# A graph attention kernel: how a small vector reaches its place, where a pass's first products and additions stand, and the order of eight banks

## The chip, the cores and the metric

The kernel runs on one core of one Trainium2 chip. The core has a matrix engine (PE, with its weight loads shown as PEld), a vector engine (DVE), a scalar engine (ACT), GpSimd (POOL) and a queue engine for transfers (SP). Each runs its own list of instructions in order, and they wait for each other through semaphores. The metric is the device time of one execution in microseconds (us). The kernel before took 2859.95 us, the median of three runs between 2857.50 and 2861.08.

## The reference

Two layers over 4096 nodes with 256 features. Each is a residual around a graph operation on h = relu(layernorm(x)).

```python
# layer 0: graph attention, 4 heads of 64
h = (h @ W).reshape(n, heads, head_dim)
src = einsum('nhd,d->nh', h, a[:head_dim, 0]);  dst = einsum('nhd,d->nh', h, a[head_dim:, 0])
e = src[:, :, None] + dst.T[None, :, :]
e = where(e > 0, e, 0.2 * e);  e = where(adj > 0, e, NEG_INF)
out = einsum('nhm,mhd->nhd', softmax(e), h)
x = x + layernorm(out) * gamma + beta
# layer 1: two steps of Xf = R @ Xf (R = row-normalised adj + I) and
# Xa = top_p(softmax(q k^T)) @ Xa, then x = x + layernorm(h + Z) * ln_g + ln_b
```

## The kernel before

Rows are taken in 32 blocks of 128. X, the features, stays on the chip. Layer 0 has two stages, both with the order of instructions written out by hand (`manual_schedule`).

**The prologue** goes through the 32 blocks once. For a block, DVE takes the row statistics (`measured`, L149 and L150), POOL makes scale and bias from them (`steps`, L141 to L144), ACT normalises and clips (`opened`, L244, hb), PE transposes (`turned_rows`, L251), ACT copies the transposes (L255, hT), and PE multiplies by wx (`multiplied`, L258). ACT and DVE then turn the product into weighted rows in three bfloat16 parts (`read`, `weighed`, `first_part`, `left`, `second_part`, `third_part`), of which the first head's stay on the chip (ut0) and the others are stored. `turn_of(b)` issues one step for several blocks at once, so that the engines overlap.

The tile wx holds W and, in its last 8 columns, W times the two halves of the vector a placed head by head. These columns are a product of w_t, the transpose of W (L575, copied at L576), and spots (L582). The tile spots is zero but for a's two halves, one column for each half and head; it is filled by four transfers issued on ACT's queue (L201), which are laid out one element per partition. Issues for the weights of layer 1 (L207 to L209) stand behind them on the same queue, and hb of block 0 behind those.

**The passes.** There are 16: four groups of eight row blocks, and in each group four heads, so that pass k belongs to group k // 4 and head k % 4. A pass has 16 pairs of source blocks. For a pair, ACT or DVE makes signs (`signs`, L371 and L373), DVE makes two masks from the signs and the adjacency (`masks`, L379 and L380), and PE adds four products for each of eight banks, 32 in all (`products`, L399). A bank is one accumulator `acc` for one row block. Signs are issued three pairs ahead of the products, and masks two. At the start of the next pass the banks are evicted, one after another, by ACT (L413) and DVE (L416), and PE begins the new pass's products into a bank once it has been read. Work that follows from an eviction (division, row statistics, the residual and the store of a finished group) is put in a list `later` and taken one piece per pair; the group's end (`closing`) falls into the next group's first-head pass.

The residual needs x + beta. The 32 additions of beta to a block of X are done on POOL (L612) during first-head passes. POOL also issues the transfers of the adjacency (L175, L551), in order with its other work.

The first pair of pass 0 stands at the end of the prologue. Its eight banks are those that the prologue uses for its own products, and one of them, bank 7, first serves to transpose the 128 source terms (`spread_all`, L564, copied at L565 into sT).

After the last pass `passing.close()` gives the eight banks back and new pools take them. PE goes on with the first hop of layer 1 (L630), then logits (L736) and attention products (L1104).

Of the kernel before, what the change touches and what calls it, by code (L numbers as in the profile page):

```python
# [11 lines left out]
F32 = mybir.dt.float32  # L12
# [14 lines left out]
P = 128  # L27
# [13 lines left out]
G0 = 8  # L41
# [15 lines left out]
def gat_then_top_p_diffusion(  # L57
# [18 lines left out]
    nc = tc.nc  # L76
    N, D = x.shape
    HD = a.shape[0] // 2
    H = D // HD
    DA = w2_t.shape[0]  # L80
    NB = N // P
    KC = D // P
# [11 lines left out]
    ident = const.tile([P, P], F32, name="ident")  # L94
# [62 lines left out]
    W3 = 3 * W1  # L157
# [4 lines left out]
    with tc.tile_pool(name="l0", bufs=1) as l0, tc.tile_pool(name="l0s", bufs=2) as l0s, tc.tile_pool(name="l0o", bufs=1) as l0o:  # L162
        passing = ctx.enter_context(ExitStack())
        l0a, l0u, l0m = (passing.enter_context(tc.tile_pool(name=x, bufs=n)) for x, n in (("l0a", 9), ("l0u", 6), ("l0m", 3)))
        pools = SimpleNamespace()
# [18 lines left out]
        def in_bank(i, shape):  # L184
            return pools.ps0.tile(shape, F32, name=f"b{i}", tag=f"acc{i}")
# [3 lines left out]
        with tc.manual_schedule(engines=every | {ET.SP}):  # L189
            wx = rp.tile([P, KC, D + 2 * H], F32, name="wx", tag="ar", bufs=4)  # L190
# [6 lines left out]
            nc.sync.dma_start(X[:, 0, :], x[:P, :])  # L197
            spots = l0.tile([P, KC, 2, H], F32, name="spots")
            nc.vector.memset(spots, 0.0)
            for h in range(H):  # L200
                nc.scalar.dma_start(spots[ds(h * HD % P, HD), h * HD // P, :, h],  # L201
                                    bass.AP(tensor=a.tensor, offset=a.offset, ap=[[1, HD], [HD, 2]]))
            nc.sync.dma_start(wx[:, :, :D], w.rearrange("(k p) d -> p k d", p=P))
            nc.sync.dma_start(X[:, 1:4, :], x[P:4 * P, :].rearrange("(b p) d -> p b d", p=P))
            for g in range(1, NB // 4):
# [20 lines left out]
            def measured(b):  # L226
                if b < NB:
                    if b % 4 == 0:
                        pro.mv = l0s.tile([P, 4, nc.vector.BN_AGGR_DIM], F32, name="mv4")
                    moments_of(pro.mv[:, b % 4, :], X[:, b, :])  # L230
                    if b == 0:
                        pro.first = [l0s.tile([P, 4], F32, name=f"{x}4") for x in ("rs", "nmr")]
                    if b < 2:
                        steps(pro.mv[:, ds(b, 1)], 1, l0s, *(t[:, ds(b, 1)] for t in pro.first))
                    if b == 3:
                        steps(pro.mv[:, 2:], 2, l0s, *(t[:, 2:] for t in pro.first))
                    elif b % 4 == 3:
                        pro.scales[b // 4] = steps(pro.mv, 4, l0s)
# [21 lines left out]
            def read(b):  # L260
                pm, uv = pro.pm[b], uvs[b % len(uvs)]
                for t, scale in enumerate((1.0, ALPHA)):
                    nc.scalar.activation(uv[:, :, t, HD:], pm[:, ds(D + H, H)][:, :, None], AF.Exp, scale=scale)
                nc.vector.tensor_scalar(sd_c[:, :, :, b], pm[:, ds(D, 2 * H)].rearrange("p (t h) -> p t h", t=2),
                                        TINY, -TINY, ALU.add, ALU.add)
# [77 lines left out]
                    mask_stage(0)  # L343

        PAIRS = NB // 2
        passes = [(ig, h) for ig in range(NB // G0) for h in range(H)]
        shared = {}
        out_rows = {}
        later = []
        lifted = list(range(NB))  # L350
# [38 lines left out]

        def products(k, p, m, banks=range(G0)):  # L390
            ig, h = passes[k]
            if p == 0 and banks[0] == 0:
                shared[k].acc = [pools.ps0.tile([P, 2, W3 + 1], F32, name=f"acc{i}") for i in range(G0)]
            cols = W3 + (h == 0)
            for i in banks:
                for c in range(2):
                    j = 2 * p + c
                    for t in range(2):
                        nc.tensor.matmul(shared[k].acc[i][:, t, :cols], m[t][:, c, ts(i, P)],  # L399
                                         shared[k].ut[j // QUARTER][:, j % QUARTER, t, :cols],  # L400
                                         start=(j == 0 and t == 0), stop=(j == NB - 1 and t == 1))

        def evacuate(k):
            ig, h = passes[k]
            acc = shared[k].acc
            if h == 0:
                out_rows[ig] = l0o.tile([P, G0, D], F32, name="o")
            st = l0o.tile([P, 4, 2 * H * (W3 + 1) // 2], F32, name="st").rearrange("p a b -> p (a b)")
            st = st[:, :G0 * 2 * W3].rearrange("p (i t k d) -> p i t k d", i=G0, t=2, k=3)
            for i in range(G0):  # L410
                b = ig * G0 + i
                one, two = (st[:, i, t].rearrange("p k d -> p (k d)") for t in range(2))
                nc.scalar.activation(two, acc[i][:, 1, :W3], AF.Copy, scale=e_c[1][:, h, b:b + 1])  # L413
                if h == 0:
                    nc.vector.reduce_sum(rinv[:, b:b + 1], acc[i][:, :, W3], axis=AX.X)
                nc.vector.scalar_tensor_tensor(one, acc[i][:, 0, :W3], e_c[0][:, h, b:b + 1], two, ALU.mult, ALU.add)  # L416

            def three():
                for n in (1, 2):
                    nc.vector.tensor_tensor(st[:, :, 0, 0], st[:, :, 0, 0], st[:, :, 0, n], ALU.add)  # L420

            def divided():
                rden = small.tile([P, G0], F32, name="rden")
                nc.vector.reciprocal(rden, st[:, :, 0, 0, HD])
                nc.vector.tensor_mul(out_rows[ig][:, :, ts(h, HD)], st[:, :, 0, 0, :HD],
                                     rden[:, :, None].to_broadcast([P, G0, HD]))
                if h == 0:
                    rs = rinv[:, ts(ig, G0)]
                    nc.vector.tensor_scalar(rs, rs, 1.0, None, ALU.add)
                    nc.vector.reciprocal(rs, rs)  # L430
            def sourced(n):
                source(hop1, n)
                split(hop1, n + 1)

            ready = []
            if k == H + 1:
                ready = [lambda n=n: sourced(n) for n in range(LOOK + 1)]
            elif k == H + 2:
                ready = [lambda n=n: edge(hop1, n) for n in range(LOOK)]
            elif k == 2 * H + 1:  # L440
                ready = [lambda n=n: own(hop1, n + 1) for n in range(LOOK)]
            return [three, divided] + ready + (closing(ig) if h == H - 1 else [])

        PASSES = NB // G0
        S = SimpleNamespace(spare=None)

        order = [(p, j) for p in range(PASSES) for j in range(NB)]

# [70 lines left out]

        todo = [(k, p) for k in range(len(passes)) for p in range(PAIRS)]  # L520
        gs, ms = {}, {}
# [47 lines left out]
        rest.update({5 + i: lambda i=i: factors(i) for i in range(2)})  # L569
        with tc.manual_schedule(engines=every):  # L570
            measured(0)
            pt = in_bank(0, [P, KC, KC, P])
            for k in range(KC):
                for c in range(KC):
                    nc.tensor.transpose(pt[:, k, c, :], wx[:, k, ts(c, P)], ident)  # L575
            nc.vector.tensor_copy(w_t, pt)  # L576
            opened(0)
            turned_rows(0)
            pm = in_bank(1, [P, KC, 2 * H])
            for k in range(KC):  # L580
                for c in range(KC):
                    nc.tensor.matmul(pm[:, k, :], w_t[:, k, c, :], spots[:, c].rearrange("p t h -> p (t h)"),  # L582
                                     start=(c == 0), stop=(c == KC - 1))
            for b in range(1, 4):
                measured(b)
            nc.vector.tensor_copy(wx[:, :, D:], pm)
            for b in range(4, 8):
                measured(b)
            opened(1)
            for b in range(NB):  # L590
                turn_of(b)
            read(NB - 1)
            weighed(NB - 1)
            mask_stage(1)
            signed(3)
            sign_stage(2)
            for n, (k, p) in enumerate(todo):
                if n > 0 and p == 0:
                    later.extend(evacuate(k - 1))
                sign_stage(n + 3)  # L600
                mask_stage(n + 2)
                if n == 0:
                    products(k, p, ms[n], range(5))
                    spread_all()
                    products(k, p, ms.pop(n), range(5, G0))
                else:
                    products(k, p, ms.pop(n))
                if n in rest:
                    rest[n]()
                if k % H == 0 and (2 if k else 7) < p < PAIRS - 1 and lifted:  # L610
                    b = lifted.pop(0)
                    nc.gpsimd.tensor_tensor(X[:, b, :], X[:, b, :], beta_r, ALU.add)  # L612
                if 1 < p < PAIRS - 3 and later:
                    later.pop(0)()
            later.extend(evacuate(k))
# [739 lines left out]
    for n in range(STEPS):  # L1355
# [4 lines left out]
        with tc.manual_schedule(engines=every):  # L1360
# [66 lines left out]
            r = blocks[NB - 1]  # L1427
# [49 lines left out]
```

## Time and profile before

| | |
|---|---|
| median of three runs | 2859.95 us |
| the profiled execution | 2860.89 us |
| its span | 2859.1 us |
| prologue, until the first product of pass 0 | 0 to 85.4 us |
| the 16 passes, about 43.8 us each | 85.4 to 786.1 us |
| layer 1, until the end | from 787.1 us |
| longest waits of PE | L258 for ACT's hT, 20.1 us in 19 waits; L575 for wx, 4.8 us |

The profile shows one execution. The span is the time between its first and last instruction. An engine's busy time is summed over its instructions; in the timeline a row gives its start, duration, engine, line, the tiles written and read, and in square brackets the idle time just before it with what ended that. A name such as ACTq or SPq is the queue in which that engine issues transfers. Equal instructions that follow each other are merged into one row with their count. Where several conditions end a wait, it is put down to the one that came last by the profile, which can be wrong where that engine had long been done.

### The profile page before, as it was taken

How to read it: one execution, taken by the hardware profiler on the slowest of the kernel's cores; microseconds unless marked ns; L12 is line 12 of the kernel's file. 1: busy time of each engine (PE TensorE's matmuls, PEld its weight loads, DVE VectorE, ACT ScalarE, POOL GpSimd, SP SyncE). 2: the span in 40 equal slices, each digit the busy share in tenths (PEclk: the TensorE clock that was granted, in tenths of full speed). 3: DMA queues.
4: the chain of work that ended last, by engine and by line, in shares of the span. 5: the costliest groups of instructions: out<-in, count | busy, mean ns of one | idle time of the engine just before them, and what ended most of it. 6: DMA issues, size and time to landing. Idle time of an engine off the chain costs nothing. (4 is left out here: it accounts for less than half of the span.)

```text
span 2859.1 us, 51521 instructions
## 1 busy us (share of the span) xinstructions
PE 2798.3 (98%) x18789; PEld 2438.7 (85%) x18789; DVE 2167.1 (76%) x5064; ACT 1919.8 (67%) x3065; POOL 870.5 (30%) x1815
## 2 busy tenths in 40 slices
PE   6999999999999999999999999999999999999998
PEld 4899999999978788888888888667778888888887
DVE  8867868778554384888888887333564999999997
ACT  7867876879533636788778884233627778877782
POOL 7402121011000121222332221000204766666664
PEclk8999999999999999999999999999999999999999
DMA  9969696686376783000000001667991111111110
GB/s 198 252 246 194 219 235 187 219 198 223 130 242 196 236 300 94 20 20 20 25 22 20 20 20 59 226 200 237 326 337 50 31 33 39 31 31 31 36 35 26
DMA packets 190811, 376.43 MB, mean 132 GB/s; under 512 B 18768, under 2 KB 143568, under 8 KB 186448
## 3 DMA queue, kind: packets, MB, share of 16 engines
q1 hardware_dynamic: 147104, 275.31, 29.2%
q0 software_dynamic: 21504, 83.89, 12.3%
q10 hardware_dynamic: 21936, 13.79, 1.5%
q8 instruction: 153, 2.51, 0.4%
q14 instruction: 114, 0.93, 0.1%
HBM read 305.48 MB, written 113.57 MB: 147 GB/s over the span
## 5 line engine op out<-in xcount | busy, mean ns | idle before, releaser
L1104 PE MATMUL acc<-X,eT 128*128 128x256 f32 x4096 | 971.7, 382 | 3.4 <-ACT eT L1098 2.8
L1104 PEld LDWEIGHTS acc<-X,eT 128*128 128x128 f32 x4096 | 738.2, 190 | 111.2 <-ACT eT L1098 31.7
L399 PE MATMUL acc<-ut,m 128*128 128x195 bf16 (+1 forms) x8192 | 698.7, 246 | 1.9 <-DVE st L416 1.4
L399 PEld LDWEIGHTS <-m 128*128 128x128 fp8e4 x8192 | 695.9, 97 | 4.6 <-DVE st L416 1.8
L373 ACT ACTIVATE g<-sr,d_big 128x1024 uint8<-128x1024 f32 x448 | 472.7, 1136 | 3.4 <-DVE m L379 3.4
L919 ACT ACTIVATE e<-mm,nm 128x1024 f32<-128x1024 f32 x256 | 286.3, 1118 | 200.6 <-PE mm L736 199.3
L1098 ACT COPY eT<-tp 128x512 f32<-128x512 f32 x512 | 297.2, 582 | 89.6 <-PE tp L1096 89.5
L1005 DVE MAX8 cand<-big 128x8 f32<-128x228 f32 (+1 forms) x1152 | 348.3, 380 | 0.0
L630 PE MATMUL mm<-ar,hl 128*128 128x512 f32 x844 | 341.1, 407 | 6.4 <-DMA ar<-adj_d 3.0
L987 DVE SCALAR_TENSOR_TENSOR big<-e,c 128x4096 f32<-128x4096 f32 x58 | 261.9, 4515 | 97.4 <-POOL c L972 58.6
L630 PE MATMUL acc<-ar,hl 128*128 128x512 f32 x844 | 328.7, 392 | 2.5 <-DVE stage L640 1.3
L943 POOL TENSOR_TENSOR sums<-sums 128x2 f32<-128x2 f32 x64 | 12.9, 202 | 1022.4 <-ACT void L926 1022.4
L1096 PE MATMUL tp<-ident,e 128*128 128x128 f32 x2048 | 306.1, 272 | 1.9 <-DVE ns_i_u L892 1.0
L1096 PEld LDWEIGHTS tp<-ident,e 128*128 128x128 f32 x2048 | 254.8, 140 | 61.2 <-DVE ns_i_u L892 1.3
L379 DVE TENSOR_TENSOR m<-g,ax 128x512 uint32<-128x512 uint32 x256 | 180.7, 706 | 110.1 <-PE acc L399 91.4
L1030 DVE SCALAR_TENSOR_TENSOR e<-e,found 128x4096 f32<-128x4096 f32 x58 | 259.2, 4468 | 0.0
L926 ACT ACTIVATE void<-e,c1x 128x2048 int8<-128x2048 f32 x128 | 257.5, 2011 | 1.3 <-DMA ar<-adj_d 0.9
L926 ACT ACTIVATE void<-e,c 128x2048 int8<-128x2048 f32 x128 | 257.5, 2012 | 0.0
L736 PE MATMUL mm<-kT,qT 128*128 128x512 f32 x512 | 198.4, 468 | 3.5 <-ACT e L919 2.5
L380 DVE TENSOR_TENSOR m<-m,ax 128x512 uint32<-128x512 uint32 x256 | 180.4, 705 | 25.3
L630 PEld LDWEIGHTS mm<-ar,hl 128*128 128x128 f32 x844 | 158.9, 188 | 45.5 <-issue 5.7
L630 PEld LDWEIGHTS acc<-ar,hl 128*128 128x128 f32 x844 | 158.9, 188 | 40.0 <-issue 4.9
(305 smaller groups left out, 3518.6 us busy)
## 6 DMA issues: line engine op xcount, KB each, us to landing
ar<-adj_d SPq DMA_DIRECT2D x211, 512.0 KB, 4.5
adj_d<-ax POOLq DMA_DIRECT2D x32, 2048.0 KB, 7.2
ut<-uv_d SPq DMA_DIRECT2D x60, 784.0 KB, 5.9
aru<-adj_d SPq DMA_DIRECT2D x45, 512.0 KB, 4.4
ax<-in_adj_t_dram POOLq DMA_DIRECT2D x32, 512.0 KB, 18.2
x<-xf_d SPq DMA_DIRECT2D x78, 128.0 KB, 4.9
xf<-xft_d SPq DMA_DIRECT2D x64, 128.0 KB, 2.2
sr<-s_d SPq DMA_DIRECT2D x15, 512.0 KB, 4.9
```

The source lines that it names most:

```text
L373: nc.scalar.activation(g[:, c, :], shared[k].sr, AF.Relu, scale=BIG, bias=d_big[:, h, j:j + 1])
L399: nc.tensor.matmul(shared[k].acc[i][:, t, :cols], m[t][:, c, ts(i, P)], shared[k].ut[j // QUARTER][:, j % QUARTER, t, :cols], start=(j == ...
L630: nc.tensor.matmul(A.acc[c][s], A.hl[m][:, t, ts(s, P)], A.ar[m][:, ts(c, 512)], start=(j == 0 and t == 0), stop=(j == NB - 1 and t == 1))
L736: nc.tensor.matmul(pm[:, h, :], q[t], kT[:, ds(h * (N // 2) + c * 512, 512)], start=(t == 0), stop=(t == 1))
L919: nc.scalar.activation(ev[:, :, c, :], r.pm[c], AF.Exp, bias=r.nm, accum_out=r.sums[:, c // 2, c % 2:c % 2 + 1])
L926: nc.scalar.activation(void, r.e[:, ts(h, N // 2)], (AF.Relu, AF.Sign)[i], bias=r.c1, scale=-1.0, accum_out=r.sums[:, h, 2 + i:3 + i])
L987: nc.vector.scalar_tensor_tensor(big, r.e, r.c3, r.e, ALU.is_le, ALU.mult, accum_out=r.low3)
L1005: nc.vector.max(cand[:, s, :], big[:, edges[s]:edges[s + 1]])
L1030: nc.vector.scalar_tensor_tensor(r.e, r.e, r.t, r.e, ALU.is_ge, ALU.mult, accum_out=kept)
L1096: nc.tensor.transpose(pt[:, i, :], r.e[:, ts(4 * g + i, P)], ident)
L1098: nc.scalar.copy(eT, pt)
L1104: nc.tensor.matmul(r.acc[:, 0, :], eT[:, i, :], cur[:, j, :], start=(j == 0), stop=(j == NB - 1))
```

## The change

It has four parts.

1. The vector a comes by one transfer into a small tile, twice: two rows (its halves), each repeated. A product with a 2x2 identity turns it so that it stands on the 128 partitions, and four copies on DVE place it in spots. The copy of the finished columns into wx moves from DVE to ACT, and its bank changes.
2. The products of pass 0's first pair into banks 0, 1, 2 are issued before the prologue's last step. Banks 3 and 4, the transposes of the source terms, and banks 5 and 6 follow at the old place; bank 7's products of this pair follow the second pair's other seven banks. An accumulator is now taken when its first product is issued.
3. The additions of beta are issued in third-head passes, at pairs 3 to 12, instead of first-head passes.
4. The last pair's products and the last eviction take the banks in the order 0, 1, 6, 7, 2, 3, 4, 5.

```diff
-            for h in range(H):
-                nc.scalar.dma_start(spots[ds(h * HD % P, HD), h * HD // P, :, h],
-                                    bass.AP(tensor=a.tensor, offset=a.offset, ap=[[1, HD], [HD, 2]]))
+            twice = l0.tile([2, 2, HD], F32, name="twice")
+            nc.scalar.dma_start(twice, bass.AP(tensor=a.tensor, offset=a.offset, ap=[[HD, 2], [0, 2], [1, HD]]))
...
+        RELEASED = (0, 1, 6, 7, 2, 3, 4, 5)
...
-            if p == 0 and banks[0] == 0:
-                shared[k].acc = [pools.ps0.tile([P, 2, W3 + 1], F32, name=f"acc{i}") for i in range(G0)]
+            if p == 0 and not hasattr(shared[k], "acc"):
+                shared[k].acc = {}
             cols = W3 + (h == 0)
             for i in banks:
+                if p == 0:
+                    shared[k].acc[i] = pools.ps0.tile([P, 2, W3 + 1], F32, name=f"acc{i}")
...
-            for i in range(G0):
+            for i in RELEASED if k == len(passes) - 1 else range(G0):
...
+        EARLY = (0, 1, 2)
...
             measured(0)
+            pa = in_bank(1, [P, 2])
+            nc.tensor.matmul(pa, twice.rearrange("t r d -> t (r d)"), ident[:2, :2], start=True, stop=True)
+            for h in range(H):
+                rows_of = ds(h * HD % P, HD)
+                nc.vector.tensor_copy(spots[rows_of, h * HD // P, :, h], pa[rows_of])
...
-            pm = in_bank(1, [P, KC, 2 * H])
+            pm = in_bank(2, [P, KC, 2 * H])
...
-            nc.vector.tensor_copy(wx[:, :, D:], pm)
+            nc.scalar.copy(wx[:, :, D:], pm)
...
-            for b in range(NB):
+            for b in range(NB - 1):
                 turn_of(b)
+            products(0, 0, ms[0], EARLY)
+            turn_of(NB - 1)
...
-                    products(k, p, ms[n], range(5))
+                    products(k, p, ms[n], (3, 4))
                     spread_all()
-                    products(k, p, ms.pop(n), range(5, G0))
+                    products(k, p, ms[n], (5, 6))
+                elif n == 1:
+                    products(k, p, ms[n], range(G0 - 1))
+                    products(k, 0, ms.pop(0), (G0 - 1,))
+                    products(k, p, ms.pop(n), (G0 - 1,))
                 else:
-                    products(k, p, ms.pop(n))
+                    products(k, p, ms.pop(n), RELEASED if n == len(todo) - 1 else range(G0))
...
-                if k % H == 0 and (2 if k else 7) < p < PAIRS - 1 and lifted:
+                if k % H == 2 and 2 < p < PAIRS - 3 and lifted:
                     b = lifted.pop(0)
                     nc.gpsimd.tensor_tensor(X[:, b, :], X[:, b, :], beta_r, ALU.add)
```

## The prediction

> **What bounds the kernel now.** I read the page's engine totals first, then the table of stages, then PE's waits, and last the timeline at the few places where PE waited beside an edited line. The totals:
>
> ```profile
> PE 2798.3 (98%) x18789; PEld 2438.7 (85%) x18789; DVE 2167.1 (76%) x5064; ACT 1919.8 (67%) x3065; POOL 870.5 (30%) x1815
> ```
>
> PE is idle for 2859.1 - 2798.3 = 60.8 us in all, so an edit outside the prologue can only win back single microseconds. Two prologue waits come first, from the timeline (start, duration, engine, line):
>
> ```profile
> 3.65 0.61 ACTq L207 DMA_DIRECT2D w_s<-in_w_t_dram  x1
> ...
> 5.82 0.38 ACTq L209 DMA_DIRECT2D wkq<-in_w_t_dram  x1
> 5.88 0.69 DVE L576 COPY w_t<-b 128x512 f32<-128x512 f32 x1 [2.28 <-PE b L575]
> 6.24 0.60 ACT L244 ACTIVATE hb<-X,nmr,rs 128x256 f32<-128x256 f32 x1 [4.22 <-DMA X<-in_x_dram]
> ...
> 9.31 1.42 PE L582 MATMUL b<-spots,w_t 128*128 128x8 f32 x6 [1.50 <-DMA spots<-in_a_dram]
> ...
> 10.40 0.60 ACT L244 ACTIVATE hb<-X,nmr,rs 128x256 f32<-128x256 f32 x1 [0.85 <-POOL nmr L144]
> ...
> 10.77 0.18 DVE L586 COPY wx<-b 128x16 f32<-128x16 f32 x1 [2.59 <-PE b L582]
> 11.06 1.38 PEld L258 LDWEIGHTS b<-wx,hT 128*128 128x128 f32 x4 [0.21 <-ACT hb L244]
> 11.09 2.10 PE L258 MATMUL b<-wx,hT 128*128 128x264 f32 x4
> ```
>
> The product with spots waits for spots' transfers. DVE, in order, waits 2.59 us behind it with the statistics of blocks 4 to 9 queued. The first hb (ready at 5.15, when POOL's nmr ends) starts at 6.24, because ACT's queue still issues L209.
>
> From 15 to 85 us DVE (67.4 us busy of 70) and ACT (62.9) set the pace together. From 85.4 to 786.1 PE does: 8192 products at 85.3 ns are 699 us. The stage table (length, then busy time of PE, PEld, DVE, ACT, POOL; clock; DMA) for passes 4, 5, 6:
>
> ```profile
> 260.70:304.50 43.80, 43.80 (x516) 43.65 (x514) 39.84 (x80) 34.72 (x43) 9.57 (x13) 1.00 0.62 143
> 304.50:348.30 43.80, 43.12 (x503) 42.27 (x503) 34.56 (x74) 36.43 (x45) 5.27 (x8) 1.00 0.62 227
> 348.30:392.10 43.80, 43.80 (x518) 43.80 (x516) 31.01 (x55) 33.68 (x43) 5.00 (x8) 1.00 0.70 239
> ```
>
> First-head pass 4 leaves DVE 4 us free, third-head pass 6 leaves it 12.8. PE loses 0.68 us at the head of pass 5. The timeline there, and at the end of the last pass:
>
> ```profile
> 302.56 1.45 DVE L379 TENSOR_TENSOR m<-g,ax 128x512 uint32<-128x512 uint32 x1
> 302.71 0.74 POOL L612 TENSOR_TENSOR X<-X,beta_r 128x256 f32<-128x256 f32 x1
> ...
> 305.26 5.91 PE L399 MATMUL acc<-ut,m 128*128 128x195 bf16 x63 [0.68 <-DVE st L416]
> ```
>
> ```profile
> 784.27 2.80 DVE L416 SCALAR_TENSOR_TENSOR st<-acc,e_c,st 128x195 f32<-128x195 f32 x8 [7.49 <-ACT st L413]
> ...
> 787.13 0.50 PE L630 MATMUL mm<-ar,hl 128*128 128x512 f32 x1 [0.97 <-DVE st L416]
> ```
>
> A mask beside a beta addition takes 1.45 us, others 0.69; the eviction queued behind it is late and PE waits. PE's waits list this release twice (1.4 us), at the heads of passes 5 and 9.
>
> [...] spots' 0.5 KB took 3.4 to 6.6 us to land, X's first 128 KB took 2.2. [...] a block's L258 takes 2.10 us at 11.09, but 1.16 at 18.68.
>
> **Part 1, the prologue's start.** Four issues of spots (2.69 us on ACT's queue) become one; SP's X loads no longer wait behind them. Twice has four rows of 256 bytes, issued near 0.9. Its landing isn't in the trace: between 2.2 us (X's first) and 3.4 (the first spots), so 3.1 to 4.3. Its product is bounded by L582's 0.22 to 0.36 us per instruction, two of them, so it ends by 5.0 at worst, and PE's queue behind it (L575, which waits for wx until 4.76) loses 0 to 0.3; I take 0. Four small copies on DVE, at the 0.16 us of sd_c's PSUM read or at most 0.35, fall into DVE's wait before 5.88: nothing, and 0.6 to 1.4 us without that cover.
>
> Then by hand. hb(0) runs 5.18 to 5.78, its transposes until 6.5 (0.67), w_t until 6.57 as before. L582 runs eight instructions at 0.24: 6.6 to 8.5, before until 10.73. Now ACT copies wx (0.2, bounded by 0.18 on DVE and 0.37 of an hT copy) to 8.75; behind it hb(1), before at 8.69, runs 8.75 to 9.35; transposes until 10.1; the first L258 starts at 10.1 instead of 11.09. So 2.2 us become 1.0, because hb(1) now queues behind the wx copy. hb(2) stays at 10.40: POOL's chain fixes it.
>
> What follows depends on the array's rate. If both first L258 stay slow (2.10, 1.97), the second ends at about 14.8 and read(1) on ACT starts at 14.85, before at 15.69: 0.85 us. If the denser PE work has brought the full rate by then (1.16 each), hb(4), now ready at 12.8 because DVE measures blocks 4 to 7 from about 8.5 to 10.8 and POOL's chain takes 2.0 more, runs then instead of at 15.18, and DVE's read(0) at 12.25 instead of 14.12: at least 1.9, say 2.0. I take the middle, **1.4 us**, ends 0.85 and 2.0. From there DVE and ACT are nearly without gaps (DVE's waits for ACT between 10 and 83 us sum to 1.7), so the shift arrives at 85 us. An end of 0 is possible if a transfer then governs, but no wait for one is shown after the first blocks.
>
> **Part 2, the three early banks.** Twelve products (1.02 us) move into PE's 2.07 us wait before the last L258 at 84.60, and bank 7 goes behind pair 1, past the 0.33 us wait for sT. But DVE's masks don't come sooner: pair 1's ends at 88.33 + 0.69 = 89.02, pair 2's at 92.10, and PE takes pair 2 at 92.16. In the new order PE waits at pair 1 until about 89.0, then does 36 products (3.07 us) and is at pair 2 at 92.1. The stall moves from pair 2 to pair 1: **0.1 us**, bounds 0 and 0.2. No queue but PE's is reordered; bank 6 still waits for block 31's weighted rows (87.5).
>
> **Part 3, beta.** The 32 additions (0.72 to 1.2 us on POOL) leave passes 0, 4, 8, 12 and stand in 2, 6, 10, 14, at pairs 3 to 12, clear of the pass heads. Without the mask's 0.76 us the evictions at 302.2 and in pass 9 are in time: 2 x 0.7 = **1.4 us**; lower bound 0.6 if the remaining DVE backlog of closing work keeps half of it. In their new place they slow masks by at most 0.76 (L379) + 0.34 (L380, 1.03 against 0.69) = 1.10 us each, ten per pass: 11.0 against 12.8 us of free DVE time in pass 6. Cost nothing; POOL's queue there holds adjacency stores and loads, which start up to 1.2 us later and have a pass of slack.
>
> **Part 4, the order of the last pair.** Evictions of banks 0, 1, 6, 7 now come first, and the hop's first tiles lie there. But in the built program the hop's first product still waits for the count that the last eviction raises: now bank 5's, at the same place. The last eviction follows the last product as before. **0**; 0.97 if the wait were by bank. After 786 us no instruction or wait differs otherwise, and PE's 98% carries the shift to the end.
>
> **Sum**: 1.4 + 0.1 + 1.4 + 0 = 2.9 us, ends of the likeliest case 1.5 and 3.8. The profiled execution took 2860.89 us around its span of 2859.1, so 2858.0; the runs' median lies 0.94 lower, at 2859.95: **2857.0 us**, own range 2856.1 to 2858.5.
>
> **Rivals.**
> 1. The head start is swallowed in the prologue (a store's slot or a half-filled ACT sets 85 us anyway) and only the pass heads gain. For it: three engines share that stage, POOL at 40.0 of 45 us between 40 and 85. Against: no transfer is waited for. Gain 0.3 to 1.5: about 2859.0.
> 2. All of it works, the hop starting at the last product too: 2.0 + 0.2 + 1.4 + 0.97 = 4.6 us, 2855.4; over 5.7 only if the prologue keeps the whole 2.6 of DVE's wait and more. Against: the wait on the last eviction.
> 3. Slower: beta additions in third-head passes push masks behind PE. Price 1.10 us per addition by the dearest rows; it decides where one costs over 12.8 / 10 = 1.28 us in pass 6, which no row shows. To overcome 2.9 and reach 0.2% needs 8.6 us over three passes, 1.57 per addition: 2866.
> That the change doesn't do what it says is certain for part 4 and nearly so for part 2; it is in the forecast.
>
> **How the numbers follow.** 0.2% is 5.7 us, about what a measurement of this kernel can tell from no change. Forecast 0.67, rival 1 0.18, rival 2 0.11 (about half beyond 0.2%), rival 3 0.04. So faster 0.06, same 0.90, slower 0.04. The range 2854.5 to 2860.2 takes in the forecast, rival 1 and most of rival 2, with the runs' spread of 3.6 us in mind.
>
> **What would show it.** Right: first L258 near 10.1; the pass heads' wait for L416 gone; a wait for m at pair 1; the 0.97 us wait at the first L630 still there; masks up to 1.5 us in passes 2, 6, 10. Wrong: the first pass's second pair starting less than 0.8 us earlier (part 1), new mask waits in third-head passes (part 3), L630 without a wait (part 4), or twice landing after 4.8.

## Result and profile after

The changed kernel takes 2851.92 us (median of 9 runs, 2850.47 to 2853.69), before 2858.61 us in the same comparison (9 runs, 2856.18 to 2861.08): ratio 0.9976, 95% interval 0.9966 to 0.9986, or 6.7 us less. A second comparison gave 0.9980 (0.9972 to 0.9988), 5.4 us between the medians. The prediction, 2857.0 us with a range from 2854.5, lies too high, and "faster by over 0.2%" is where the medians of the first comparison fall (0.24%) and at the edge of the second (0.20%).

The profiled execution took 2850.95 us around a span of 2849.2. The engine totals of the page after (busy time, share of the span, instructions):

```profile
PE 2796.1 (98%) x18791; PEld 2441.2 (86%) x18791; DVE 2174.5 (76%) x5067; ACT 1918.8 (67%) x3066; POOL 861.3 (30%) x1815
```

PE is now idle for 2849.2 - 2796.1 = 53.1 us, 7.7 less than before. The prologue's start, from the timeline (start, duration, engine, line, operation; in brackets the idle time before and what ended it):

```profile
2.37 0.60 ACTq L208 DMA_DIRECT2D wkq<-in_w_t_dram  x1
...
2.44 0.58 PE L576 MATMUL b<-ident,twice 2*128 2x2 f32 x2 [2.44 <-POOL ident masks.py:199]
...
3.50 0.64 DVE L579 COPY spots<-b 64x2 f32<-64x2 f32 x4
...
4.10 1.12 PE L583 MATMUL b<-ident,wx 128*128 128x128 f32 x4 [1.07 <-DMA wx<-in_w_dram]
5.16 0.60 ACT L243 ACTIVATE hb<-X,nmr,rs 128x256 f32<-128x256 f32 x1 [3.13 <-POOL nmr L144]
5.25 0.69 DVE L584 COPY w_t<-b 128x512 f32<-128x512 f32 x1 [1.11 <-PE b L583]
...
6.29 1.72 PE L590 MATMUL b<-spots,w_t 128*128 128x8 f32 x8
...
8.04 0.17 ACT L594 COPY wx<-b 128x16 f32<-128x16 f32 x1 [2.29 <-PE b L590]
8.11 0.60 ACT L243 ACTIVATE hb<-X,nmr,rs 128x256 f32<-128x256 f32 x1
...
9.25 1.96 PE L257 MATMUL b<-wx,hT 128*128 128x264 f32 x4
```

ACT's queue has issued its last weights at 2.97 instead of 6.20, the eight products with spots run without a break, and the first value product starts at 9.25 instead of 11.09. The block's four products take 1.96 us there, nearly as long as the first two blocks of before (2.10 and 1.97 us, against 1.16 for the block at 18.68). The passes 4, 5, 6 by stage (length, then busy time of PE, PEld, DVE, ACT, POOL; clock; DMA share; GB/s):

```profile
258.56:302.11 43.55, 43.55 (x514) 43.55 (x513) 39.13 (x90) 34.47 (x42) 3.90 (x6) 1.00 0.66 160
302.11:345.67 43.56, 43.56 (x515) 43.56 (x514) 33.53 (x68) 37.42 (x48) 5.23 (x8) 1.00 0.58 212
345.67:389.22 43.55, 43.55 (x514) 43.55 (x513) 36.54 (x55) 33.66 (x42) 12.04 (x18) 1.00 0.71 241
```

PE is never idle in them. DVE's work in pass 6 grew from 31 to 36.5 us, POOL's from 5 to 12. The timeline at the head of pass 5, where no product waits:

```profile
298.79 7.39 PE L401 MATMUL acc<-ut,m 128*128 128x196 bf16 x85
...
299.23 0.69 DVE L380 TENSOR_TENSOR m<-m,ax 128x512 uint32<-128x512 uint32 x1
```

And the timeline at the end of the last pass, where the hop's first product waits as it did:

```profile
779.50 2.80 DVE L418 SCALAR_TENSOR_TENSOR st<-acc,e_c,st 128x195 f32<-128x195 f32 x8 [7.49 <-ACT st L415]
...
782.35 0.50 PE L644 MATMUL mm<-ar,hl 128*128 128x512 f32 x1 [0.97 <-DVE st L418]
```

The hop's first product is a good landmark, because from there on both kernels give PE the same 10378 products and transposes in the same order. It starts at 782.35 instead of 787.13: 4.8 us. The two spans differ by 9.9, so 5.2 us more fell behind it (2066.8 us from there to the end, against 2072.0). Matching the instructions one by one shows where: not a drift, but steps, with level stretches between. The larger ones are 1.2 us in the hop's first 160 products, at waits for adjacency rows; 0.4 near 994 us, mostly at a logits product that waits for ACT; and 2.8 in the last hop, of which 1.6 stand at waits for rows or for DVE's work on one. The last 1.2 us, near 2101, don't come from a longer wait: PE waits 1.8 us for a row there in the kernel before and 1.7 in the changed one. But in the profile of before the products behind that wait start 0.43 us apart instead of 0.23, in a stretch with a granted clock of 0.50. From that profile (stretch, length, busy time of PE, PEld, DVE, ACT, POOL; clock; DMA share; GB/s):

```profile
2098.29:2101.70 3.41, 1.60 (x7) 1.05 (x6) 1.65 (x4) 0.41 (x1) 0.00 (x0) 1.00 0.95 326
2101.70:2105.11 3.41, 3.41 (x9) 2.62 (x8) 3.26 (x6) 0.41 (x1) 0.00 (x0) 0.50 0.98 331
```

No instruction there was changed. So two questions were open: which edit makes which part of the 4.8, and whether the 5.2 belongs to the change at all.

### The profile page after: what moved, and what is told of

It reads as the page before. It is cut to its first block, busy times and chain, and to the rows that moved or that the text cites. A ratio compares the mean times of both kernels' runs of the same rounds, so it can differ in the third digit from the quotient of the medians.

```text
span 2849.2 us, 51524 instructions
## 1 busy us (share of the span) xinstructions
PE 2796.1 (98%) x18791; PEld 2441.2 (86%) x18791; DVE 2174.5 (76%) x5067; ACT 1918.8 (67%) x3066; POOL 861.3 (30%) x1815
## 3 DMA queue, kind: packets, MB, share of 16 engines
q10 hardware_dynamic: 21366, 13.79, 1.5%
## 5 line engine op out<-in xcount | busy, mean ns | idle before, releaser
L379 DVE TENSOR_TENSOR m<-g,ax 128x512 uint32<-128x512 uint32 x256 | 188.9, 738 | 97.3 <-PE acc L401 76.8
```

## Experiments

Most verdicts rest on the landmark and on the lengths of the sixteen passes (from the start of each pass's first product), and the times on many runs only confirm them. How exact are they? The lengths of passes 1 to 15 repeat within 0.04 us wherever their code is the same. The landmark repeats less well, because the prologue does: pass 1 starts between 129.76 and 130.20 us in the six profiles that have before's first transfers, so a difference of 0.3 us at the hop decides nothing by itself.

**The kernel before, unchanged, profiled again.**

> The kernel before, unchanged, profiled a second time. The two profiles at hand differ by 9.9 us: 4.8 up to the first hop product (782.35 against 787.13) and some 4.9 inside the hops, at single waits for adjacency rows (the first pass of the first hop 1.2 us, later in that hop 0.4, the last hop 2.8). Theory (those hop waits differ from one execution to the next): this profile starts the hop at 787.1 again, within 0.1, but its waits for adjacency rows differ from those of the first profile by a us or more. Rival (the hop waits belong to the kernel before and are removed by the change): they return here with the same places and lengths, and this profile ends within 1 us of 2860.9. Ratio of times 1.000 either way.

Ratio 0.9997 (0.9989 to 1.0005). The hop starts at 786.95, every pass has its length of the first profile within 0.03 us, and the rest takes 2069.7 instead of 2072.0. From PE's waits in the stretch of the first layer's hops (775 to 1130 us), the line for adjacency rows (us in total, times, longest) of the first profile of before:

```profile
PE mm L630 <- DMA ar<-adj_d: 2.4, 2, 1.7
```

And the same line of this profile:

```profile
PE mm L630 <- DMA ar<-adj_d: 1.8, 3, 0.8
```

The same code waits 2 times for 2.4 us and then 3 times for 1.8, at other products. Up to the hop these two profiles agree within 0.2 us; behind it they don't.

**The first edit alone.** Before with these lines of the change and no others:

```diff
-            for h in range(H):
-                nc.scalar.dma_start(spots[ds(h * HD % P, HD), h * HD // P, :, h],
-                                    bass.AP(tensor=a.tensor, offset=a.offset, ap=[[1, HD], [HD, 2]]))
+            twice = l0.tile([2, 2, HD], F32, name="twice")
+            nc.scalar.dma_start(twice, bass.AP(tensor=a.tensor, offset=a.offset, ap=[[HD, 2], [0, 2], [1, HD]]))
...
+            pa = in_bank(1, [P, 2])
+            nc.tensor.matmul(pa, twice.rearrange("t r d -> t (r d)"), ident[:2, :2], start=True, stop=True)
+            for h in range(H):
+                rows_of = ds(h * HD % P, HD)
+                nc.vector.tensor_copy(spots[rows_of, h * HD // P, :, h], pa[rows_of])
...
-            pm = in_bank(1, [P, KC, 2 * H])
+            pm = in_bank(2, [P, KC, 2 * H])
...
-            nc.vector.tensor_copy(wx[:, :, D:], pm)
+            nc.scalar.copy(wx[:, :, D:], pm)
```

> Before with the first edit alone: the two-row tile, the product that turns it, the four copies into spots, and wx's copy on ScalarE. Theory (the weights land earlier, 4.10 us for 4.76, as the 512 small pieces of the four transfers are gone): the first value product starts near 9.25 instead of 11.09, the prologue's last step moves by 2.3 us, the first hop product is at 784.8; time 2.3 us below before, plus or minus what the hops' waits do. The prediction had 1.4 us here. Rival (the 2.3 us needs the other edits too): 1.4 or less, hop at 785.7.

Ratio 0.9987 (0.9980 to 0.9993). The hop starts at 784.99: 2.0 us of the 4.8. The first value product starts at 9.53, not at 9.25, and wx landed at 4.39, not 4.05, so the reason given in the expectation was already in doubt. The traces show another one. In all six profiles with before's start of the prologue the first value product starts 1.91 us after the last of the four column transfers landed (8.81 to 9.18 us). In the five with the two-row tile and nothing else on ACT's queue it starts 5.14 to 5.20 us after wx landed. So before, the columns set this start, and after the edit wx does.

**Beta's move alone.** One line of before:

```diff
-                if k % H == 0 and (2 if k else 7) < p < PAIRS - 1 and lifted:
+                if k % H == 2 and 2 < p < PAIRS - 3 and lifted:
```

> Before with the beta additions moved to third-head passes, nothing else. Theory (both the 0.84 us waits at the heads of passes 5 and 9 and the slow first 32 products after each, 0.40 us, go): all passes last 43.56 us, the first hop product is at 787.13 - 2.48 = 784.65; time 2.5 us less. The prediction had 1.4. Rival (the 0.40 us comes back elsewhere): hop at 785.7.

Ratio 0.9991 (0.9983 to 0.9999). The hop starts at 784.56, 2.5 us earlier, and passes 1 to 14 all take 43.55 or 43.56 us. In before, passes 4 and 8 took 44.40 and passes 5 and 9 43.95. So a late eviction cost 0.84 + 0.40 us each time, not the 0.68 that the waits list. Both differences can be read in the trace of before. The products start 0.085 us apart but each record lasts 0.25, so a break of 0.93 us from start to start (304.33 to 305.26) shows as an idle time of 0.68, and is worth 0.93 - 0.085 = 0.84. After it every bank's first product waits for its own eviction: DVE's reads of the first four banks end at 305.21, 305.61, 305.99 and 306.39, and the first products into them start at 305.26, 305.66, 306.05 and 306.45. That is a bank each 0.394 us, where four products need 0.340, and over eight banks it comes to 0.4, in pieces too short to show as idle time.

**The changed kernel with beta put back** (the same line the other way).

> The changed kernel with the beta additions back in the first-head passes. Theory: it loses what the move gives, 2.48 us, in the same two places: passes 4 and 5 and passes 8 and 9 are longer by 0.84 and 0.40 us, first hop product at 782.35 + 2.48 = 784.8; time 2.5 us above the changed kernel, about 4.2 below before. Rival (without the prologue's delay the same waits don't form): no long passes, hop at 782.35.

Ratio to before 0.9986 (0.9979 to 0.9992). Hop at 784.48, 2.1 us later than in the changed kernel's first profile and 2.4 than in its second; passes 4, 5, 8, 9 are 44.38, 43.95, 44.39, 43.94 again. The move's gain doesn't depend on the other edits.

**Beta in first-head passes still, but two pairs less at the end.**

```diff
-                if k % H == 0 and (2 if k else 7) < p < PAIRS - 1 and lifted:
+                if k % H == 0 and (2 if k else 7) < p < PAIRS - 3 and lifted:
```

> Before with the beta additions still in the first-head passes, but not in the last two pairs that had them (p below PAIRS - 3 in place of PAIRS - 1; what is left moves to pass 12). Theory A (the addition beside the last masks of a pass delays VectorE into the evictions): the long passes 4, 5, 8 and 9 fall back to 43.56 us, hop at 784.6. Theory B (first-head passes have too much VectorE work of their own, 39.8 us against 30 in other passes, so that the additions cost wherever they lie in them): passes 4 and 5 and 8 and 9 stay long by 0.84 and 0.40 us, hop at 787.

Ratio 0.9996 (0.9987 to 1.0004), but the lengths decide: passes 4 and 8 fall to 43.56, passes 5 and 9 to 43.68 and 43.66; the hop starts at 784.45. Its profile at the end of pass 4 shows the same mask as before's, now without an addition beside it, and the eviction in time:

```profile
302.56 0.69 DVE L380 TENSOR_TENSOR m<-m,ax 128x512 uint32<-128x512 uint32 x1
303.24 0.41 DVE L416 SCALAR_TENSOR_TENSOR st<-acc,e_c,st 128x195 f32<-128x195 f32 x1
```

Theory A holds but for 0.1 us a pass: it was the last one or two additions before a pass's end, not the passes' load. The four passes got 2.2 us shorter together; the rest of the shift at the hop is the prologue, which ended 0.3 us earlier in this profile than in the others, in unchanged code. In time this version is not distinguished from before: 2.2 us would be a ratio of 0.9992, which the interval takes in.

**The early banks alone, and the last pair's order alone.** Each on before, everything else left. The first makes pair 0's products for banks 0 to 2 inside the prologue, for banks 3 to 6 in the loop and for bank 7 after pair 1, as in the change:

```diff
+            products(0, 0, ms[0], EARLY)
...
+                elif n == 1:
+                    products(k, p, ms[n], range(G0 - 1))
+                    products(k, 0, ms.pop(0), (G0 - 1,))
+                    products(k, p, ms.pop(n), (G0 - 1,))
```

The second:

```diff
-            for i in range(G0):
+            for i in RELEASED if k == len(passes) - 1 else range(G0):
...
-                    products(k, p, ms.pop(n))
+                    products(k, p, ms.pop(n), RELEASED if n == len(todo) - 1 else range(G0))
```

> Before with the early banks alone: pair 0's products for banks 0 to 2 inside the prologue, bank 7's after pair 1's. Theory: the stalls for the first masks are only spread over pairs 0 and 1, and the end of pair 2 stays where pair 2's own mask puts it; first hop product within 0.2 us of 787.0 (787.13 and 786.95 so far), time within 2 us of before. Rival (it is this edit that shortens the first 160 products of the first hop, 38.2 to 38.3 us in the two kernels with it and 39.1 to 39.7 in the others): that stretch reads 38.3.

> Before with the last pair's banks and their evictions in the released order alone. Theory (the pool's end is waited for, whatever the order): the first hop product still waits 0.97 us and starts at 787.0 within 0.2; time within 2 us of before. Rival (the order lets the hop run on): the wait is below 0.6 us, or the hop's first 160 products take 38.3 us instead of 39.1 to 39.7.

Ratios 1.0002 (0.9993 to 1.0011) and 0.9998 (0.9989 to 1.0007). The hop starts at 786.75 and 786.99, with its 0.97 us wait in both. The first 160 products of the hop took 38.1 and 38.4 us, so both rivals seemed right at once; the changed kernel profiled again (39.0) showed that this stretch just varies.

The early banks' 786.75 lies 0.27 us below the mean of 787.02 for before, before again and the order alone, and just outside the 0.2 that was expected. It isn't their gain. In all fourteen profiles, with the early banks or without, the first product that reads pair 2's second mask starts 0.06 us after this mask's end, and pass 1 starts 38.09 to 38.10 us after it. So the mask sets the pace either way. What moved is the prologue ahead of it: its first value product started at 10.89 there, at 11.03 to 11.09 in the other three.

The ledger: the first edit brings 2.0 us at the hop in its own profile, and 2.2 at the start of pass 1 as the mean of five profiles that have it with no columns on that queue (127.84) against six without it (130.02). The early banks bring 0, beta 2.5, the order 0. That is 4.7 in sum with the means, and 4.8 was measured (782.35 and 782.11 against 787.02); the difference is within the prologue's scatter.

**The four column transfers kept**, into a tile that nobody reads, in the changed kernel; once ahead of the two-row transfer and once behind it:

```diff
+            unread = l0.tile([P, KC, 2, H], F32, name="unread")
+            nc.gpsimd.memset(unread, 0.0)
+            for h in range(H):
+                nc.scalar.dma_start(unread[ds(h * HD % P, HD), h * HD // P, :, h],
+                                    bass.AP(tensor=a.tensor, offset=a.offset, ap=[[1, HD], [HD, 2]]))
```

> The changed kernel with the four column transfers of before kept, into a tile that nobody reads, ahead of the two-row transfer on the same queue. Theory [...]: the weights land at 4.7 again instead of 4.10, the first value product moves from 9.25 by 0.6 us, and the first hop product from 782.35 to 782.9. Rival (wx lands earlier for another reason, the waits on ScalarE's or SyncE's queue): the weights land at 4.10 and the hop starts at 782.35.

> The changed kernel with the four column transfers kept, into a tile that nobody reads, this time behind the two-row transfer. In before wx landed at 4.09 to 4.87 in six profiles and the third column at 8.3 to 9.0, and the product that reads it started at 8.95 to 9.31. Theory (only the wait of the products for the columns cost time, not the traffic of their pieces): wx lands between 4.0 and 4.9, the first value product follows it by 5.2 us, and the hop starts within 0.5 us of 782.4. Rival (the queue's time on ScalarE, four issues of 0.65 us[...] cost as well): first value product at 10 or later, hop at 783 or later.

The first: ratio to before 0.9996 (0.9988 to 1.0005), hop at 786.41. It told less than meant, as the two-row transfer, fifth on its queue, was issued at 4.61 and landed only near 8.46, and the weights' transposes stand behind its product on PE. But wx itself landed at 4.03. With the four transfers under way (0.5 KB each; their queue, q10 of the page, carried 21936 packets in before and 21366 in the changed kernel) it was no later than without them: the theory, 4.7, fell. In the eight profiles of kernels with the four transfers (the next one included), wx landed at 4.62, 4.31, 4.87, 4.09, 4.16, 4.69, 4.03 and 4.02, without them at 4.39, 4.22, 4.05, 4.30, 4.25: it varies by itself.

The second: ratio 0.9992 (0.9985 to 0.9998), hop at 785.25, 2.9 to 3.1 us later than without the four transfers, with wx at 4.02 and the two-row tile in time. Its timeline:

```profile
1.85 2.71 ACTq L205 DMA_DIRECT2D unread<-in_a_dram  x4
...
4.60 2.04 ACTq L211 DMA_DIRECT2D w_s<-in_w_t_dram  x1
...
4.80 0.19 POOL L144 TENSOR_TENSOR nmr<-nmr,rs 128x1 f32<-128x1 f32 x1
...
7.51 0.49 ACTq L213 DMA_DIRECT2D wkq<-in_w_t_dram  x1
8.05 0.60 ACT L248 ACTIVATE hb<-X,nmr,rs 128x256 f32<-128x256 f32 x1 [6.03 <-POOL nmr L144]
...
9.19 1.72 PE L595 MATMUL b<-spots,w_t 128*128 128x8 f32 x8
```

The first hb could run at 5.0, when nmr is there, and stands until 8.05 behind ACT's own issues: four of columns, then three of weights that are slow or wait. From the first to the last of these three it takes 3.40 us, in the other seven profiles with columns ahead of them 2.49 to 2.91, and 1.60 to 1.61 in the six without. (The idle time is put down to nmr, which had long been done.) So the rival holds: the four transfers cost time with nobody waiting for their data. A part of the hold belongs to the experiment: the first of the four stands until 1.85 for the clearing of its tile on POOL, though the two-row transfer was issued by 1.33, so up to 0.5 us of it is not the transfers' own. In before it is both: hb is held from 5.15 to 6.24, and the third of the product instructions with spots to 9.31, which is 0.13 us after the fourth column's landing. There the landing comes last and sets the pace.

**A step further: three pools in place of one.** The first product of the hop waits for the last of eight evictions although its own bank is freed first. In the built kernel it is one pool that closes. In this version the eight banks lie in three pools, each of them the place of one kind of the hop's tiles:

```diff
-        pools.ps0 = passing.enter_context(tc.tile_pool(name="ps0", bufs=1, space=PSUM))
+        banks_of = ((0, 1, 2, 3), (4, 5), (6, 7))
+        opened_ps = [passing.enter_context(tc.tile_pool(name=f"ps0{x}", bufs=1, space=PSUM)) for x in "abc"]
+        pools.ps0 = {i: pool for pool, group in zip(opened_ps, banks_of) for i in group}
...
-        RELEASED = (0, 1, 6, 7, 2, 3, 4, 5)
+        RELEASED = (0, 1, 2, 3, 6, 7, 4, 5)
...
+        ps4 = ctx.enter_context(tc.tile_pool(name="ps4b", bufs=2, space=PSUM))
```

The new pool takes all tiles named mm of the later stages.

> The changed kernel with the eight accumulator banks in three pools instead of one (banks 0-3, 4-5, 6-7, each the place of one of the hop's own kinds of tiles), and the last pair's order 0 1 2 3 6 7 4 5. Theory (it is the closing of the one pool that holds the hop's first product to the last of the eight evictions): the product waits for bank 3's eviction alone, the 0.97 us wait falls to 0.2 or less, and the hop starts 0.8 to 1.0 us earlier; time 0.8 us under the changed kernel. Rival (what is late next takes the place, the adjacency rows of the hop's first 160 products): the hop starts earlier but the 160 products take 0.8 us longer, no gain.

Ratio 0.9977 (0.9969 to 0.9986), 2853.97 us beside 2854.14 of the changed kernel in the same comparison. The timeline at the hop:

```profile
781.28 0.48 PE L647 MATMUL mm<-ar,hl 128*128 128x512 f32 x1
...
781.79 0.19 PEld L647 LDWEIGHTS acc<-ar,hl 128*128 128x128 f32 x1 [0.34 <-DVE st L420]
```

The 0.97 us wait is gone, as the theory has it, with 0.34 left at the second product; the hop starts 0.8 to 1.1 us earlier. The length of pass 15 says it more exactly, here and in the next run: 43.50 us instead of 44.69 in all other profiles. No gain in time can be told: the first 160 products took 39.5 us (38.3 and 39.0 in the changed kernel), with 1.35 us of wait at one product, for a row of adjacency that landed 0.14 us before it. That fits the rival, but a stretch that varies by 1.5 us can't prove it.

**The same with wx's transfer ahead of x's first block.**

```diff
+            nc.sync.dma_start(wx[:, :, :D], w.rearrange("(k p) d -> p k d", p=P))
-            nc.sync.dma_start(X[:, 0, :], x[:P, :])
...
-            nc.sync.dma_start(wx[:, :, :D], w.rearrange("(k p) d -> p k d", p=P))
+            nc.sync.dma_start(X[:, 0, :], x[:P, :])
```

> The same with wx's transfer issued ahead of the first block of x on SyncE's queue. Theory (the first value product follows wx's landing by 5.15 us: four transposes, the copy to w_t, eight products, the copy to wx, the first block's transposes): wx lands about 0.4 us earlier, the block of x as much later without being late, and the hop starts 0.4 us earlier than in the run before it. Rival (block x and its moments are then last): no gain, or 0.3 us of loss.

Ratio 0.9979 (0.9969 to 0.9988), and the hop 1.0 us later (782.30). wx lands at 3.69, but block 0 at 4.14 instead of 2.9, its hb runs at 6.39, and the first value product at 10.68. The rival holds, with a loss of 1.0 instead of 0.3: in the changed kernel the first block's moments and hb set the pace together with the weights.

**The changed kernel again.**

> The changed kernel once more, profiled a second time. Theory (the 5.2 us that its first profile won behind the first hop product, 2066.8 us to the end against 2072.0, are executions' own): first hop product at 782.35 within 0.4 (as wx lands between 4.0 and 4.9), and 2068 to 2071 us from there to the end, like the kernels run so far; time 4.6 to 5 us under before by the landmarks, ratio 0.9983. Rival (the change also shortens what follows): 2067 us again, ratio 0.9976 as first measured.

Ratio 0.9980 (0.9972 to 0.9988). Hop at 782.11, 2068.3 us behind it. From the hop to the end the fourteen profiles, with the same products, read from 2066.8 (the changed kernel's first, the least of all) to 2073.2, with a standard deviation of 1.9; before's first, 2072.0, is the third longest. So at least most of the 5.2 us is the luck of two executions.

A good part of this luck goes with the granted clock. Apart from one at the very end, seven profiles show no stretch of 3.41 us at a granted clock of 0.50 (half clock) behind the hop and take 2066.8 to 2069.7 us (mean 2068.5). Four show one (2069.2 to 2072.0, mean 2070.9), and three show two (2071.2 to 2073.2, mean 2072.5). By an estimate from its length and its clock of 0.50, a stretch costs up to 1.7 us; the rest of the differences is waits. Within a profile all of them begin a whole number of 3.41 us apart, those of its prologue, up to 2800 us away, included. So one can cut each trace behind the hop into such windows. In the ten windows just before a stretch at half clock, PE and its weight loads stood idle for 1.75 to 2.83 us; in some 8400 other windows at full clock, for 1.77 at most. (In the prologue the same cut doesn't part them: 1.16 to 1.89 us is found on both sides.) The wait near 2100 us, 1.1 to 2.9 us in all fourteen, is about as long, and a window's edge cuts it differently from one execution to the next: in before's first profile the edge lies 0.75 us behind the wait's end, at 2100.95, in the changed kernel's first at the wait's end, 2092.56. The second profile of before has the same wait, 1.8 us. It kept its full clock, where before's first did not:

```profile
2097.10:2100.51 3.41, 1.61 (x7) 1.06 (x7) 3.36 (x6) 0.41 (x1) 0.00 (x0) 1.00 1.05 360
2100.51:2103.92 3.41, 3.41 (x16) 2.74 (x16) 2.88 (x6) 0.88 (x3) 0.00 (x0) 1.00 1.03 402
```

Four kernels with the changed prologue have such stretches too (the three pools two; the changed kernel with beta put back, the columns kept behind, and wx first one each), so they are no mark of the kernel before.

Whether a part of the 5.2 us, up to some 2, comes with the change is left open: 4.8 us is a ratio of 0.9983, inside both intervals, but both medians lie beyond it (6.7 and 5.4). The mean granted clock was 0.995 or less in 1 of the changed kernel's 23 timed runs and in 47 of before's 142 in the later comparisons, so such stretches might be rarer in it. But this mean takes in the prologue, and the three pools have 4 of 13, so that isn't shown.

## Why the prediction was wrong

It was 5.1 us too high (2857.0 against 2851.92), in three parts. 1.3 us is the base: the three first runs of before had a median of 2859.95, the nine of the comparison 2858.61. 1.9 us is the sum itself: 2.9 was predicted, 4.8 measured at the hop. 1.9 us is what the comparison shows beyond the hop's landmark, not settled, as said. The sum's own upper end should have read 3.6, not 3.8 (2.0 + 0.2 + 1.4 + 0); 4.8 lies beyond both.

**Part 3 (1.4 us; measured 2.5) is the term that failed most.** The mechanism was right: the mask beside an addition, the late eviction, the two places. The failing step is "the evictions at 302.2 and in pass 9 are in time: 2 x 0.7 = 1.4 us". It took the price from the idle time in the waits, which is 0.16 us short for each wait since the products overlap in the records (0.25 us long, 0.085 apart), and it left out the 0.40 us in which PE follows DVE's evictions bank by bank. Both could have been read from before's profile: passes 4, 5, 8, 9 last longer than 43.56 us by 2.5 us in all.

**Part 1 (1.4, ends 0.85 and 2.0; measured 2.0 to 2.2)** was taken at the middle of two cases, where the upper end was met, though by neither case's road. That the upper end fits is luck. "The first L258 starts at 10.1" came at 9.53 (alone) and 9.25: "w_t until 6.57 as before" leaned on wx's landing of one profile, which moves by 0.8 us from one to the next. The two-row tile came sooner than "3.1 to 4.3", as its product runs from 2.44 in the changed kernel's first profile and 2.61 in its second; nothing later waited for it. "If both first L258 stay slow ... 0.85 us": both did (1.96 us each), yet the factors sd_c of block 1 came at 13.71 instead of 15.94. The sum had laid block 1's transposes behind the first value product; they ran beside its end (11.01 to 11.64, second value product at 11.44), as they had in before (12.98 to 13.61, second at 13.41). And hb(4) ran at 12.36 in place of 15.18 without the full rate (1.16 us for a block) that the step had made its condition. That denser PE work brings this rate was the author's estimate: PE was busy for 5.13 us of the first 10 instead of 2.69, and the first two blocks still took 1.96 each; the third, at 13.62, took 1.17. What the prediction had right: the cover of the four copies, hb at 5.18, eight products without a break, and hb(1) behind the wx copy. "hb(2) stays at 10.40" was nearly right: it ran at 10.26 on the mean of six profiles with before's start and at 9.95 on that of five with the changed one, while wx's mean landing fell by 0.2, from 4.46 to 4.24.

**Part 2 (0.1, bounds 0 and 0.2; measured 0)** was right, with its mechanism: after the change PE waits for masks in pairs 0 and 1 (1.1 us) and shows no wait at pair 2, whose product still follows its mask by 0.06 us as before.

**Part 4 (0)** was right, with its reason: 0.97 us stayed, at the last eviction, and went when the pool was split.

**Rival 3, slower masks in the new place,** had the price right and the form wrong. The additions don't stand one beside a mask: POOL comes to them late, behind an adjacency store that waits for a mask, and does six in a row. From the timeline of pass 6 after:

```profile
361.78 0.71 POOL L552 COPY now<-m 128x1 fp8e4<-128x1 fp8e4 x1 [9.74 <-DVE m L379]
...
362.70 5.03 DVE L379 TENSOR_TENSOR m<-g,ax 128x512 uint32<-128x512 uint32 x1
363.02 4.16 POOL L626 TENSOR_TENSOR X<-X,beta_r 128x256 f32<-128x256 f32 x6
```

One mask takes 5.03 us, beside all six and against 0.69 without one, over three times the 1.5 us that the prediction gave as a sign of being right. The ten additions made the masks of pass 6 take 28.4 us in sum instead of 22.1, so 0.63 us each, under the 1.10 that was allowed. PE never waited, since the masks run two pairs ahead. A pair's mask is ready some time before the products that read it; after pass 0 the least such lead was 1.12 us, against 0.46 in before, and behind the row of six in pass 6 it was 1.30. At 0.69 us an addition, one more in that row would by this estimate still have fitted, two not. In both places it is the mask, the earlier of the two instructions, that takes longer: this one starts 0.32 us before the first addition, and the one at 302.56 in before (1.45 us) 0.15 us before its addition.

**Rival 2** (all of it works, 4.6 us) came nearest in its size, by another sum: 2.2 + 0 + 2.5 + 0. It had counted 0.97 for the hop's wait, which stayed, and 1.4 for beta, so its agreement is luck. The chance of 0.06 for faster by over 0.2% rested on the 2.9 and on taking the spread of runs as the only doubt about the base.

## What to carry to other kernels

Price a stall by the length of the loop that contains it against its undisturbed neighbours, not by the idle time in front of one instruction: products that overlap hid 0.16 us of each wait here, and PE, restarted behind the stall, ran at DVE's pace for eight banks, 0.394 us a bank instead of 0.340. A transfer's price in the prologue was also the issuing engine's time, 2.69 us of ScalarE for the four columns: ask what stands behind the issues on that queue, even if nobody waits for the data. And compare profiles at a landmark up to which they repeat, since the stretch from the hop to the end moved by 6.4 us (2066.8 to 2073.2) in unchanged code. Better than one landmark is the stretch between an event and what waits for it: the landmark scattered by some tenths of a us, while the 38.1 us from a mask to the next pass, the same to 0.01, showed that one edit brought nothing.

## What was not expected of the hardware

- The same code from the hop to the end took 2066.8 to 2073.2 us in fourteen profiles, the waits for adjacency rows moving between products, while the lengths of the passes before it repeat within 0.04 us.
- Behind the hop, the granted clock of PE read 0.50 for 3.41 us ten times in the fourteen profiles, each time just after a window of 3.41 us in which PE and its weight loads had stood idle for 1.75 to 2.83 us. In the some 8400 other windows at full clock the longest idle time was 1.77. Seven profiles have no such stretch, four one and three two.
- An issue of a transfer on ScalarE took 0.67 us on the mean of the four columns in before (0.62 to 0.72), 0.56 us for the two-row tile. Three issues of weights behind four such columns took 2.5 to 3.4 us together, in one profile 2.04 for a single one, and 1.6 us without columns ahead.
- One DVE mask took 5.03 us beside six GpSimd additions in a row, 4.3 us longer than the usual 0.69. Beside another row of six, at 284 us in before, DVE's instructions with two inputs came through one by one, at 0.84 to 1.16 us each.
